# Convolutional attention block, one core: vectors placed by products, two loads moved to SP's queue, and three taps moved behind a Newton step

## The chip, the cores and the metric

The kernel runs on one core of one Trainium2 chip. The time is the device time of the whole program in microseconds (us), as the median of several runs. The engines are TensorE (PE: matrix products; PEld is its weight load), VectorE (DVE), ScalarE (ACT), GpSimd (POOL) and SyncE (SP). DMAs are issued by SP, ACT and POOL.

## What is computed

The reference, cut to the lines that matter (x is 4 x 384 x 48 x 48 in fp32, 8 heads of 48 channels, N = 2304 positions):

```python
local = conv_general_dilated(x, conv_w, ..., feature_group_count=C)   # 7 x 7, depthwise
inv = bn_gamma * rsqrt(bn_var + BN_EPS)
local = local * inv + (bn_beta - bn_mean * inv)
x_norm = layernorm(x_flat, ln_gamma, ln_beta)
q, k, v = split(x_norm @ qkv_w.T + qkv_b)
q = q + layernorm(local_flat, ln_gamma, ln_beta)
attn = softmax(q @ k.T * hd ** -0.5)
out = x_flat + (attn @ v) @ proj_w.T + proj_b
```

## The kernel before

Channels lie on the 128 partitions in three chunks, in a packed order: rows 0 to 47 and 64 to 111 of chunk c hold heads 2c and 2c+1, and rows 48 to 63 and 112 to 127 hold sixteen channels each of the heads 6 and 7. A load into that order takes four DMAs (`load_packed`, L114).

An image has six groups of 384 positions for keys and values (`from_x`), and five groups of 8 or 10 image rows for queries; t counts the query groups over the four images (0 to 19). For each t there are twelve slots s: each scores six blocks of 128 keys (`score`, L1105; each score is three products of high and low parts), exponentiates on ACT (L1113) and sums the values (`weigh`, L1120). The 7 x 7 convolution of group t + 1 runs meanwhile on VectorE, tap by tap (L340), as one long stream; `convolve_first(n)` takes the next n taps of it in the first stage, and `plan` shares out what is left over the slots.

The instructions of TensorE, VectorE, ACT and SP stand in the order in which they are written. GpSimd's order is made by a scheduler after the first loads. A DMA that comes eight after another waits until that one has landed, on the hardware queues (SP and ACT together) and on GpSimd's queue alike.

The first stage (image 0, up to the first score at 163 us) does this:

- SP loads the batch norm vectors (`norms`), the slab (image rows with a border of three) of query group 0 in two parts, between them the weights `staged` of values, keys and queries, and then x of groups 1 to 5 (`load_x`).
- ACT's queue loads the taps (`taps_in`), and with GpSimd's queue the layer norm gain and shift (`of_ln`), piece by piece in packed order (`load_by_pair`, L194 and L196). GpSimd's queue also loads `qk_vec` (bias of queries and keys), `vbp` (bias of values), `pb` (output bias), the slab of group 1 and `w_o`, the output weights. Its scheduler puts one piece of `w_o` and one of the slab among its first instructions.
- `warm` issues 14 products of constants (L1163). Group 0 is then normalised in three blocks: mean (L694), centre on VectorE (L609), squares on ACT (L556), mean of the squares, root on ACT (L617 to L619), a Newton step on VectorE (L631, L632), scale (L689). Between blocks, `pack` (L244) brings taps and shift from natural into packed order by products with 0/1 matrices (`packing`), and ACT copies the result to `vec` (L251).
- `scale_values` and `scale_rows` multiply the weights by the gain (L905, L912, L913). `shift_rows` (L868) makes rows from the layer norm shift and the weights, and `columns` (L894) turns them into columns that are added to the biases (`key_bias`, `query_bias`).
- Groups 1 to 5 follow in a loop; each is normalised one turn ahead. `copies_in` (L361) makes shifted copies of the slab of group 1 with 16 DMAs on SP; `products` (L415, in the turn of group 2) does one chunk of its convolution on TensorE. `stack_head` (L717 to L720, SP) and `stored_head` and its like (L728 to L757, POOL) store the keys. In the last turn (group 5) the norm of the convolved group 0 ends (`local_end`, L942), `query_end` (L954) makes the first queries and `low_queries` (L973) splits them; its DMAs (L978, L980) put the rows where the scores need them.

At t = 0 the queries of t = 1 are made in slot 10: mean of the centred squares on TensorE (L694, after the sums of slot 9), root, Newton step, `local_end`, `query_end`, `low_queries` with six DMAs on SP.

Of the kernel before, what the change touches and what calls it, by code (L numbers as in the profile page):

```python
# [10 lines left out]
F32 = mybir.dt.float32  # L11
# [5 lines left out]
P = 128  # L17
NH = 8
HD = 48
# [29 lines left out]
def unshifted_pass(  # L49
# [16 lines left out]
    nc = tc.nc  # L66
    B, C, N = x.shape
    W = 48
    H = N // W
    CC = C // P  # L70
# [3 lines left out]
    NP = NH // 2  # L74
# [6 lines left out]
    GM = max(ROWS) * W  # L81
# [11 lines left out]
    const = ctx.enter_context(tc.tile_pool(name="const", bufs=1))  # L93
# [12 lines left out]
    def two_banks(name="r"):  # L106
        return ps.tile([P, 2, 512], F32, tag="r", name=name)
# [4 lines left out]
    def load_packed(dst, src, queue=nc.sync):  # L112
        for p0, piece in segments(src):
            queue.dma_start(out=dst[p0 : p0 + piece.shape[0]], in_=piece)  # L114
# [30 lines left out]


    T0 = KS * KS
    natural = work.tile([P, GM], F32, tag="qt", name="natural", bufs=1)[:, 0 : CC * (T0 + 1)]
    natural = natural.rearrange("p (c v) -> p c v", c=CC)
    norms = const.tile([P, 4, CC], F32, tag="norms", name="norms")  # L150
    vec = const.tile([P, CC, T0 + 1], F32, tag="vec", name="vec")
    cw, shift = vec[:, :, 0:T0], vec[:, :, T0]
    of_ln = const.tile([P, 2, CC], F32, tag="of_ln", name="of_ln")
    gain, beta = of_ln[:, 0], of_ln[:, 1]
    inv = const.tile([P, CC], F32, tag="inv", name="inv")
    neg_half = const.tile([P, CC], F32, tag="neg_half", name="neg_half")
    qk_vec = const.tile([P, 2, CC], F32, tag="qk_vec", name="qk_vec")
# [29 lines left out]
    taps_in = piece(CC, T0)  # L187
    nc.scalar.dma_start(out=taps_in, in_=conv_w)

    def load_by_pair(dst, src, queues):  # L190
        with nc.allow_non_contiguous_dma(reason="a few vectors, once"):
            for j, queue in enumerate(queues):
                r = 64 * j
                queue.dma_start(out=dst[r : r + HD], in_=src[j, :, :, 0:CC])  # L194
                for c in range(CC):
                    queue.dma_start(  # L196
                        out=dst[r + HD : r + 64, :, c], in_=src[j, 16 * c : 16 * c + 16, :, CC]
                    )

    load_by_pair(of_ln, ln_pair, (nc.scalar, nc.gpsimd))  # L200
    staged = [
        work.tile([P, CC, GM], F32, tag="qs", name="staged", bufs=5)[:, :, :C] for _ in range(3)
    ]
# [22 lines left out]
    for c, r, cc, r0, n in pieces:  # L226
        nc.vector.tensor_copy(
            packing[:, pairs.index((c, cc)), r : r + n], ident[:, r0 : r0 + n]
        )

    nc.vector.tensor_mul(inv, inv, norms[:, 0])
    nc.vector.tensor_mul(natural[:, :, T0], norms[:, 2], inv)
    nc.vector.tensor_sub(natural[:, :, T0], norms[:, 1], natural[:, :, T0])
# [3 lines left out]
        )  # L237

    def pack():
        m = two_banks()[:, 0, 0 : CC * (T0 + 1)].rearrange("p (c v) -> p c v", c=CC)  # L240
        for c in range(CC):
            mine = [pair for pair in pairs if pair[0] == c]
            for pair in mine:
                nc.tensor.matmul(  # L244
                    m[:, c, :],
                    lhsT=packing[:, pairs.index(pair), :],
                    rhs=natural[:, pair[1], :],
                    start=pair == mine[0],
                    stop=pair == mine[-1],
                )  # L250
        nc.scalar.copy(vec, m)  # L251
# [13 lines left out]
    ]  # L265
    for g in range(1, NG):
        load_x(0, g, nc.sync)
    load_by_pair(qk_vec, qk_b, (nc.gpsimd, nc.gpsimd))
    with nc.allow_non_contiguous_dma(reason="a few vectors, once"):
        load_packed(vbp, v_b.rearrange("o c -> c o"), nc.gpsimd)  # L270
    nc.gpsimd.dma_start(out=pb, in_=proj_b)
    loads.close()

# [583 lines left out]
    rows = {}  # L859

    def of_row(i):
        return slice(32 * i, 32 * i + 1)

    def shift_rows():
        r = two_banks()
        for c in range(CC):
            for i in range(3):
                nc.tensor.matmul(  # L868
                    r[of_row(i), 0, :C],
                    lhsT=beta[:, c : c + 1],  # L870
                    rhs=staged[i][:, c, :],
                    start=c == 0,
                    stop=c == CC - 1,
                )
        rows.update((i, r[of_row(i), 0, :C]) for i in range(3))

    def rows_out():
# [36 lines left out]

    def key_bias(m):
        nc.vector.tensor_add(qkb[:, 1, :], qk_vec[:, 1, :], m[1])
        nc.vector.tensor_add(vbp[:, :, 0], vbp[:, :, 0], m[2])

    def query_bias(m):

# [232 lines left out]
    def convolve_first(n):  # L1153
        nonlocal n_first
        n_first += n
        for _ in range(n):
            next(stream)


    def warm(n):  # L1160
        m = two_banks()[:, 0, 0:P]
        for _ in range(n):
            nc.tensor.matmul(m, lhsT=mean_w, rhs=ident, start=True, stop=True)  # L1163

    warm(WARM)

    blocks = [slice(i * P, (i + 1) * P) for i in range(NB)]
    raw = slabs[0, 0][0]
# [5 lines left out]
    for i, at in enumerate(blocks):  # L1174
        norm.mean_of(norm.buf, at)
        norm.root(at)
        norm.scale(norm.newton(at), at)
        scale_values(*((0,), (1, 2), ())[i])
        if i == 1:
            pack()  # L1180
            convolve_first(2)
    for c in range(CC):
        scale_rows(1, c)
# [21 lines left out]
    convolve_first(5)  # L1205
    norm.mean_by_chunk(norm.buf)
    norm.root()
    load_slab(0, 1)
    load_packed(w_o, proj_wT, nc.gpsimd)
    both(making)  # L1210
    convolve_first(4)
    lows_out(1)
# [7 lines left out]
    for g in range(1, NG):  # L1220

        last = g == NG - 1
        making = from_x(0, g)
        both(making)
        if last:
            added = output_bias()
        else:
            norm.mean_in_place()
            convolve_first(6)
        if g in (3, 5):  # L1230
            keep_stack(0, g // 2 - 1)
        norm.centre()
        norm.squares()
        if last:
            convolve_first(3)
            norm.sum_squares()
            convolve_first(3)
        both(making)
        if last:
            norm.mean_in_place()  # L1240
        else:
            if g == 1:
                taps_out()
            if g == 2:
                products()
                convolve_first(24)
            convolve_first(5)
            norm.sum_squares()
            both(making)
            norm.mean_in_place()  # L1250
        norm.root()
        if last:
            convolve_first(9)
            local_end(0, norm.newton())
            query_end(0, True)
            both(making)
            low_queries(0, 0, nc.scalar)
            convolve_first(2)
            lows_out(1)
            both(making)  # L1260
            convolve_first(4)
            both(making)
            continue
        lows_out(1)
        both(making)
        convolve_first(6)
        lows_out(2)
        norm.scale(norm.newton())
        if g == 1:
            taps_spread()  # L1270
        both(making)
        if g == NG - 2:
            assert n_first >= each
            norm = Norm(accs[0])
            norm.mean_by_chunk(norm.src)
        if g < NG - 2:
            norm = Norm(xn[0, g + 2])
            norm.sum()
        convolve_first(5)
# [6 lines left out]
    for t in range(NT):  # L1286
# [74 lines left out]
        for s in range(NSLOT):  # L1361
# [64 lines left out]
                between.extend(norm.root_jobs())  # L1426
                between.popleft()()
            if early and s == first + (2 if t == 0 else 3):
                low_queries(t + 1, 0)
            convolve("slot", t, s, 1)  # L1430
            if t and early and s == first + 2:
                local_end(t + 1, norm.newton())
# [588 lines left out]
```

## Time and profile before

| | before |
|---|---|
| median of 3 runs | 2739.66 us (2739.60 to 2740.39) |
| profiled execution | 2739.04 us |
| its span | 2737.2 us |
| TensorE / VectorE / ACT / GpSimd busy | 2714.7 / 2314.8 / 1671.1 / 603.9 us |
| matmuls | 16438 records |
| HBM read / written | 258.14 / 64.14 MB |

The profile is of one execution. Busy time counts the instructions of an engine; a matmul of fp32 data makes two records. Timelines give start and length in us, the engine, the line of the kernel, the operation, out<-in with partitions and elements, and in brackets the idle time before it and what ended it. A line can be that of a helper (L694 is `project`, L114 `load_packed`), so the names tell the instructions apart.

### The profile page before, as it was taken

The page shows a single profiled execution, that of the slowest core. Times are in us where ns is not written, and L with a number is a line of the kernel's source. Part 1 is how long each engine was busy: PE and PEld are TensorE (multiplying, and loading weights), DVE is VectorE, ACT ScalarE, POOL GpSimd, SP SyncE. Part 2 cuts the span into 40 slices and gives each one's busy share as a digit, 9 for nine tenths or more (in the row PEclk, how much of TensorE's full clock was granted, in tenths as well). Part 3 has the DMA queues.
Part 4 walks back from the last instruction along what each step waited for, and adds up shares of the span by engine and source line. Part 5 has one row for each costly group of instructions (what it writes and reads, how often), then busy time and mean ns, then how long its engine had stood idle before and what let it go on. Part 6 is the DMA issues. An engine that isn't in the chain of part 4 may idle for free.

```text
span 2737.2 us, 46047 instructions
## 1 busy us (share of the span) xinstructions
PE 2714.7 (99%) x16438; PEld 1536.6 (56%) x16438; DVE 2314.8 (85%) x4038; ACT 1671.1 (61%) x2317; POOL 603.9 (22%) x1077
## 2 busy tenths in 40 slices
PE   8999999999999999999999999999999999999999
PEld 5565555555556555555555655555555565555555
DVE  7999999989999999989889999889888998986212
ACT  4356777777325777777622677777752377776762
POOL 5541101102453111011155211111225511110110
PEclk9999999999999999999999999999999999999999
DMA  8354544446465545354555553545635544444442
GB/s 164 85 143 136 142 115 129 124 136 182 101 160 154 139 120 146 115 152 124 143 140 138 166 147 110 142 126 141 152 105 158 147 140 133 139 132 132 139 150 68
DMA packets 160223, 370.46 MB, mean 135 GB/s; under 512 B 58672, under 2 KB 107472, under 8 KB 159984
## 3 DMA queue, kind: packets, MB, share of 16 engines
q0 software_dynamic: 71424, 279.04, 35.6%
q1 hardware_dynamic: 83248, 78.33, 12.6%
q10 hardware_dynamic: 5312, 10.06, 1.1%
q8 instruction: 132, 2.16, 0.3%
q14 instruction: 107, 0.88, 0.1%
HBM read 258.14 MB, written 64.14 MB: 118 GB/s over the span
## 4 chain that ended last, share of the span: by engine, by line
PE 90%; DVE 5%; DMA 4%; ACT 0%; issue 0%; SPq 0%; POOL 0%; DVEq 0%; POOLq 0%; ACTq 0%
PE o L1120 42%; PE r L1105 34%; PE r L694 13%; DVE acc L340 2%; DMA parts<-part 1%; DMA staged<-in_qkv_wT_dram 1%; DVE k L804 0%; DMA slab<-in_x_dram 0%; PE r L415 0%; DMA four<-parts 0%; DVE xn L689 0%; DMA wide<-k 0%; DMA xn<-in_x_dram 0%; DMA out_dram<-xr 0%; DVE xr L1086 0%
## 5 line engine op out<-in xcount | busy, mean ns | idle before, releaser
L340 DVE SCALAR_TENSOR_TENSOR acc<-slab,vec,acc 128x470 f32<-128x470 f32 (+10 forms) x2832 | 1658.1, 658 | 2.0 <-ACT acc L303 2.0
L1113 ACT ACTIVATE pt<-r 128x960 f32<-128x960 f32 (+1 forms) x1440 | 1248.6, 943 | 246.4 <-PE o L1120 151.8
L1120 PE MATMUL o<-pt,v 128*64 128x480 f32 (+1 forms) x5760 | 1166.2, 554 | 0.4 <-ACT pt L1113 0.4
L1105 PE MATMUL r<-qs,ks 64*128 64x480 f32 (+1 forms) x8640 | 967.0, 373 | 4.8 <-ACT xn L818 3.0
L1105 PEld LDWEIGHTS r<-qs,ks 64*128 64x128 f32 x8640 | 785.2, 184 | 268.2 <-issue 171.6
L1120 PEld LDWEIGHTS o<-pt,v 128*64 128x64 f32 x5760 | 392.5, 137 | 659.9 <-issue 566.5
L766 POOL DMA_DIRECT2D ks<-wide x220 | 160.0, 727 | 1369.7 <-PE r L1105 1310.0
L694 PE MATMUL r<-xn,w_qk 128*128 128x384 f32 x864 | 284.7, 487 | 0.0
L997 ACT COPY o<-o 113x480 f32<-113x480 f32 (+1 forms) x160 | 87.1, 544 | 277.3 <-PE o L1120 276.7
L694 PEld LDWEIGHTS r<-xn,w_qk 128*128 128x128 f32 x864 | 164.4, 191 | 115.3 <-issue 1.8
L694 PE MATMUL r<-w_v,xn 128*128 128x384 f32 x432 | 145.3, 489 | 2.8 <-DVE xn L689 1.4
L788 ACT COPY v<-r 128x384 f32<-128x384 f32 x72 | 32.0, 479 | 183.3 <-PE r L694 183.3
L1016 DVE TENSOR_TENSOR ao<-ao,o 113x480 f32<-113x480 f32 (+1 forms) x120 | 75.9, 633 | 73.9 <-ACT o L997 73.9
L694 PEld LDWEIGHTS r<-w_v,xn 128*128 128x128 f32 x432 | 81.1, 190 | 62.6 <-DVE xn L689 3.8
L973 DVE TENSOR_TENSOR qs<-xn,qs 128x480 fp32r<-128x480 f32 (+1 forms) x60 | 38.1, 635 | 63.8 <-ACT qs L968 63.8
L751 POOL DMA_DIRECT2D wide<-k x144 | 72.4, 505 | 78.3 <-ACT k L801 64.2
L694 PE MATMUL r<-af,w_o 128*128 128x384 f32 (+1 forms) x270 | 85.2, 470 | 0.0
L1007 ACT COPY ao<-o 113x480 f32<-113x480 f32 (+1 forms) x60 | 32.6, 544 | 72.1 <-PE o L1120 72.1
L1016 DVE TENSOR_TENSOR aot<-aot,o 113x480 f32<-113x480 f32 (+1 forms) x40 | 25.4, 634 | 56.9 <-ACT o L997 56.9
L818 ACT ACTIVATE xn<-r,qkb 128x384 f32<-128x384 f32 x72 | 39.6, 576 | 50.8 <-PE r L694 47.6
L1086 DVE SCALAR_TENSOR_TENSOR xr<-r,pb,xr 128x384 f32<-128x384 f32 (+2 forms) x72 | 42.0, 611 | 33.2 <-PE r L694 26.0
L694 PEld LDWEIGHTS r<-af,w_o 128*128 128x128 f32 x270 | 51.3, 190 | 31.9
(148 smaller groups left out, 1354.9 us busy)
## 6 DMA issues: line engine op xcount, KB each, us to landing
ks<-wide POOLq DMA_DIRECT2D x220, 768.0 KB, 4.9
qs<-qs SPq DMA_DIRECT2D x352, 60.0 KB
slab<-in_x_dram POOLq DMA_DIRECT2D x24, 432.0 KB, 7.2
wide<-k POOLq DMA_DIRECT2D x96, 96.0 KB, 2.2
wide<-ks POOLq DMA_DIRECT2D x12, 768.0 KB, 5.3
xr<-in_x_dram POOLq DMA_DIRECT2D x16, 576.0 KB, 5.6
rb<-rden SPq DMA_DIRECT2D x32, 270.0 KB
held<-ao POOLq DMA_DIRECT2D x12, 720.0 KB, 3.9
```

What stands on the lines that cost most here:

```text
L340: nc.vector.scalar_tensor_tensor(dst, src, weight, dst, ALU.mult, ALU.add)
L694: nc.tensor.matmul(dst, lhsT=weights(c), rhs=src(c), start=c == 0, stop=c == CC - 1)
L751: nc.gpsimd.dma_start(out=last[16 * u : 16 * u + 16, 0], in_=k[r : r + 16, 0])
L766: queue.dma_start(out=place_keys(b, p, i), in_=wide[b, p][:, :, at])
L818: nc.scalar.activation(src[:, i, :], q[:, :G], AF.Identity, bias=qkb[:, 0, i : i + 1])
L973: nc.vector.tensor_sub(qs[:, 1, :], query_of(t, p), qs[:, 0, :])
L997: nc.scalar.copy(part[0 : 64 + HA], sums[0 : 64 + HA, 0, :n])
L1016: nc.vector.tensor_add(dst, dst, part[0 : 64 + HA])
L1086: nc.vector.scalar_tensor_tensor(xr[:, co, :], m, pb[:, co : co + 1], xr[:, co, :], ALU.add, ALU.add)
L1105: nc.tensor.matmul(r[:, j, :n], lhsT=ks[rows, w, at], rhs=qs[rows, m, :], start=i == 0, stop=i == 2,)
L1113: nc.scalar.activation(pt, r[:, :, :n], AF.Exp, scale=SCALE)
L1120: nc.tensor.matmul(sums[halves[j], 0, : columns_of(t)], lhsT=values[t // NA, kb // NB][:, first : first + 64], rhs=pt[:, j, :], start=i == ...
```

## The change

It does six things. The layer norm vectors, the query and key biases and the value bias are loaded by contiguous rows on ACT's queue into a corner of the start-up buffer, and `proj_b` moves to ACT's queue as well. Gain and shift become two more columns of `natural`, which `pack` places with the taps (52 columns instead of 50 a chunk); `pack` moves ahead of the first norm, right behind `warm`. `bias_rows` (VectorE) builds 0/1 rows and `bias_out` (four products and a copy on ACT) places the query and key biases. The value bias is added as one more product at the end of `shift_rows`. The slab of group 1 moves from GpSimd's queue to SP's, behind x of group 2, and `w_o` to SP's behind x of group 5. In the last turn of the first stage the taps ahead of the Newton step go from 9 to 6, those behind it from 2 + 4 to 3 + 6; and at t = 0 half of the DMAs of `low_queries` for t = 1 go to GpSimd's queue instead of SP's.

```diff
--- before.py
+++ after.py
@@ -145,13 +145,12 @@
 
 
     T0 = KS * KS
-    natural = work.tile([P, GM], F32, tag="qt", name="natural", bufs=1)[:, 0 : CC * (T0 + 1)]
+    natural = work.tile([P, GM], F32, tag="qt", name="natural", bufs=1)[:, 0 : CC * (T0 + 3)]
     natural = natural.rearrange("p (c v) -> p c v", c=CC)
     norms = const.tile([P, 4, CC], F32, tag="norms", name="norms")
-    vec = const.tile([P, CC, T0 + 1], F32, tag="vec", name="vec")
+    vec = const.tile([P, CC, T0 + 3], F32, tag="vec", name="vec")
     cw, shift = vec[:, :, 0:T0], vec[:, :, T0]
-    of_ln = const.tile([P, 2, CC], F32, tag="of_ln", name="of_ln")
-    gain, beta = of_ln[:, 0], of_ln[:, 1]
+    gain, beta = vec[:, :, T0 + 1], vec[:, :, T0 + 2]
     inv = const.tile([P, CC], F32, tag="inv", name="inv")
     neg_half = const.tile([P, CC], F32, tag="neg_half", name="neg_half")
     qk_vec = const.tile([P, 2, CC], F32, tag="qk_vec", name="qk_vec")
@@ -187,17 +186,13 @@
     taps_in = piece(CC, T0)
     nc.scalar.dma_start(out=taps_in, in_=conv_w)
 
-    def load_by_pair(dst, src, queues):
-        with nc.allow_non_contiguous_dma(reason="a few vectors, once"):
-            for j, queue in enumerate(queues):
-                r = 64 * j
-                queue.dma_start(out=dst[r : r + HD], in_=src[j, :, :, 0:CC])
-                for c in range(CC):
-                    queue.dma_start(
-                        out=dst[r + HD : r + 64, :, c], in_=src[j, 16 * c : 16 * c + 16, :, CC]
-                    )
-
-    load_by_pair(of_ln, ln_pair, (nc.scalar, nc.gpsimd))
+    of_ln = piece(2, CC)
+    nc.scalar.dma_start(out=of_ln, in_=ln)
+    biases = piece(2, NP)
+    nc.scalar.dma_start(out=biases[0 : 2 * HD], in_=qk_b.rearrange("j d v p -> (j d) v p"))
+    of_values = piece(C)[64:65]
+    nc.scalar.dma_start(out=of_values, in_=v_b)
+    nc.scalar.dma_start(out=pb, in_=proj_b)
     staged = [
         work.tile([P, CC, GM], F32, tag="qs", name="staged", bufs=5)[:, :, :C] for _ in range(3)
     ]
@@ -228,6 +223,7 @@
             packing[:, pairs.index((c, cc)), r : r + n], ident[:, r0 : r0 + n]
         )
 
+    nc.vector.tensor_copy(natural[:, :, T0 + 1 : T0 + 3], of_ln.rearrange("p v c -> p c v"))
     nc.vector.tensor_mul(inv, inv, norms[:, 0])
     nc.vector.tensor_mul(natural[:, :, T0], norms[:, 2], inv)
     nc.vector.tensor_sub(natural[:, :, T0], norms[:, 1], natural[:, :, T0])
@@ -237,7 +233,7 @@
         )
 
     def pack():
-        m = two_banks()[:, 0, 0 : CC * (T0 + 1)].rearrange("p (c v) -> p c v", c=CC)
+        m = two_banks()[:, 0, 0 : CC * (T0 + 3)].rearrange("p (c v) -> p c v", c=CC)
         for c in range(CC):
             mine = [pair for pair in pairs if pair[0] == c]
             for pair in mine:
@@ -265,11 +261,40 @@
     ]
     for g in range(1, NG):
         load_x(0, g, nc.sync)
-    load_by_pair(qk_vec, qk_b, (nc.gpsimd, nc.gpsimd))
-    with nc.allow_non_contiguous_dma(reason="a few vectors, once"):
-        load_packed(vbp, v_b.rearrange("o c -> c o"), nc.gpsimd)
-    nc.gpsimd.dma_start(out=pb, in_=proj_b)
+        if g == 2:
+            load_slab(0, 1, queue=nc.sync)
+    load_packed(w_o, proj_wT)
     loads.close()
+
+    chosen_rows = spread_taps[1][:, 2 * 448 : 2 * 448 + 4 * P].rearrange("p (a m) -> p a m", m=P)
+
+    def bias_rows():
+
+        rows = chosen_rows.rearrange("p a (j x) -> p a j x", j=2)
+        nc.vector.memset(chosen_rows, 0.0)
+        nc.vector.tensor_copy(
+            rows[:, 0, :, 0:HD], ident[:, 0 : 2 * HD].rearrange("p (j d) -> p j d", j=2)
+        )
+        nc.vector.tensor_copy(
+            rows[:, 1:4, :, HD:64],
+            ident[:, 0 : 2 * HD].rearrange("p (j c r) -> p c j r", j=2, c=CC),
+        )
+
+    def bias_out():
+        m = two_banks()[:, 0, 0 : 2 * CC].rearrange("p (v c) -> p v c", v=2)
+        rows = slice(0, 2 * HD)
+        nc.tensor.matmul(
+            m, lhsT=chosen_rows[rows, 0, :], rhs=biases[rows, :, 0:CC], start=True, stop=False
+        )
+        for c in range(CC):
+            nc.tensor.matmul(
+                m[:, :, c],
+                lhsT=chosen_rows[rows, 1 + c, :],
+                rhs=biases[rows, :, CC],
+                start=False,
+                stop=c == CC - 1,
+            )
+        nc.scalar.copy(qk_vec, m)
 
 
 
@@ -870,8 +895,11 @@
                     lhsT=beta[:, c : c + 1],
                     rhs=staged[i][:, c, :],
                     start=c == 0,
-                    stop=c == CC - 1,
+                    stop=c == CC - 1 and i != 2,
                 )
+        nc.tensor.matmul(
+            r[of_row(2), 0, :C], lhsT=one[of_row(2)], rhs=of_values, start=False, stop=True
+        )
         rows.update((i, r[of_row(i), 0, :C]) for i in range(3))
 
     def rows_out():
@@ -914,7 +942,7 @@
 
     def key_bias(m):
         nc.vector.tensor_add(qkb[:, 1, :], qk_vec[:, 1, :], m[1])
-        nc.vector.tensor_add(vbp[:, :, 0], vbp[:, :, 0], m[2])
+        nc.vector.tensor_copy(vbp[:, :, 0], m[2])
 
     def query_bias(m):
 
@@ -1163,6 +1191,8 @@
             nc.tensor.matmul(m, lhsT=mean_w, rhs=ident, start=True, stop=True)
 
     warm(WARM)
+    pack()
+    bias_rows()
 
     blocks = [slice(i * P, (i + 1) * P) for i in range(NB)]
     raw = slabs[0, 0][0]
@@ -1177,7 +1207,7 @@
         norm.scale(norm.newton(at), at)
         scale_values(*((0,), (1, 2), ())[i])
         if i == 1:
-            pack()
+            bias_out()
             convolve_first(2)
     for c in range(CC):
         scale_rows(1, c)
@@ -1205,8 +1235,6 @@
     convolve_first(5)
     norm.mean_by_chunk(norm.buf)
     norm.root()
-    load_slab(0, 1)
-    load_packed(w_o, proj_wT, nc.gpsimd)
     both(making)
     convolve_first(4)
     lows_out(1)
@@ -1250,15 +1278,15 @@
             norm.mean_in_place()
         norm.root()
         if last:
-            convolve_first(9)
+            convolve_first(6)
             local_end(0, norm.newton())
             query_end(0, True)
             both(making)
             low_queries(0, 0, nc.scalar)
-            convolve_first(2)
+            convolve_first(3)
             lows_out(1)
             both(making)
-            convolve_first(4)
+            convolve_first(6)
             both(making)
             continue
         lows_out(1)
@@ -1426,7 +1454,7 @@
                 between.extend(norm.root_jobs())
                 between.popleft()()
             if early and s == first + (2 if t == 0 else 3):
-                low_queries(t + 1, 0)
+                low_queries(t + 1, 0, nc.gpsimd if t == 0 else nc.sync)
             convolve("slot", t, s, 1)
             if t and early and s == first + 2:
                 local_end(t + 1, norm.newton())
```

## Prediction

> **What bounds the kernel now.** The page first: TensorE is busy nearly all the time, so a change pays only where TensorE is idle, runs at a reduced clock, or has work taken away.
>
> ```profile
> span 2737.2 us, 46047 instructions
> PE 2714.7 (99%) x16438; PEld 1536.6 (56%) x16438; DVE 2314.8 (85%) x4038; ACT 1671.1 (61%) x2317; POOL 603.9 (22%) x1077
> ```
>
> 2737.2 - 2714.7 = 22.5 us of idle time. The waits of TensorE (total, times, longest) say that over half of it lies before 165 us:
>
> ```profile
> PE r L1105 <- ACT xn L818: 3.0, 1, 3.0
> PE r L1163 <- POOL mean_w L165: 2.8, 1, 2.8
> PE r L694 <- DMA xn<-in_x_dram: 2.8, 1, 2.8
> PE r L694 <- issue: 2.5, 1, 2.5
> ```
>
> The timeline of TensorE places them (start, length; in brackets the idle time before and its releaser):
>
> ```profile
> 10.60 3.70 PE L694 MATMUL r<-slab,mean_w 128*128 128x128 f32 x18 [2.50 <-issue]
> 14.14 1.50 PE L694 MATMUL r<-sq,mean_w 128*128 128x128 f32 x12
> 15.48 1.66 PE L244 MATMUL r<-natural,start_up 128*128 128x50 f32 x14
> 26.41 2.10 PE L694 MATMUL r<-xn,w_qk 128*128 128x384 f32 x6
> 32.53 4.18 PE L694 MATMUL r<-xn,mean_w 128*128 128x384 f32 x6 [2.76 <-DMA xn<-in_x_dram]
> 36.50 4.56 PE L694 MATMUL r<-xn,w_qk 128*128 128x384 f32 x12
> ```
>
> Six records of 128x384 take 2.10 us at 26.41 and 4.18 at 32.53: after each idle stretch the clock is halved. The table by stretch of time has it (third column from the end is the clock):
>
> ```profile
> 10.00:12.00 2.00, 1.40 (x6) 1.43 (x7) 0.00 (x0) 0.00 (x0) 1.01 (x2) 0.56 1.11 156
> 32.00:34.00 2.00, 1.47 (x3) 0.90 (x4) 0.77 (x2) 0.00 (x0) 1.02 (x2) 0.50 1.03 189
> ```
>
> The last two columns are DMA, saturated at 156 to 189 GB/s: two loads hold TensorE up, the fourth piece of the first slab (0,0) and group 1 of x. VectorE waits with it (3.97 us, then 1.36 us):
>
> ```profile
> 36.74 0.16 DVE L921 TENSOR_TENSOR qkb<-qk_vec,r 128x3 f32<-128x3 f32 x1 [3.97 <-PE r L694]
> 44.82 0.62 DVE L631 SCALAR_TENSOR_TENSOR sq<-r,eps,sq 128x384 f32<-128x384 f32 x1 [1.36 <-ACT sq L619]
> ```
>
> GpSimd's timeline shows who shares the DMA engines: loads that nobody needs before 47.9 us (the slab of group 1) and 143 us (w_o):
>
> ```profile
> 1.44 0.74 POOL L114 DMA_DIRECT2D w_o<-in_proj_wT_dram  x1 [0.38 <-issue]
> 5.06 0.65 POOL L114 DMA_DIRECT2D slab<-in_x_dram  x1
> ```
>
> [...] in the first 12 us GpSimd's queue takes 36.9% of the engines and SP's 47.4%. [...] 674 of the 1552 packets of those 12 us are under 512 B. [...] here 2.50 and 2.76 us were enough and 0.93 us (at 259.4) was not, so I use the trace.
>
> **The change, part by part.**
>
> Fewer DMAs ahead (POOL). GpSimd loses 25 issues; ACT keeps five, all contiguous rows now. Bytes ahead of x group 1 on SP: slab 576 KB, weights 1728, slab's rest 216, x 576: 3.17 MB. GpSimd adds 1152 + 576 KB = 1.77 MB. At 165 GB/s (table, 12 to 24 us) from 2.0 us: 21.2 us alone, 31.9 with GpSimd's; it landed at 32.4. So group 1 should land near 22 to 23 us. The slab: its fourth piece is issued at 5.08, when the first has landed, and lands at 10.5; 648 KB of w_o and slab lie between, up to 4 us, so it should land at 6.5 to 8.
>
> Start of TensorE. The mean weights come after one DMA issue less (0.74) and five memsets more (0.37): 0.4 earlier. The warm-up (5.31) ends at 7.7. pack() now comes here, 1.66 us, to 9.35. It needs `natural`, ready at 7.74 before; its chain was behind 2.1 us of GpSimd issues, now gone, and two vectors on ACT's queue. bias_rows (memset by the 896-column one's 0.81 us: 0.46; two copies, up to 0.4) fits VectorE's 4.53 us of waiting. So the means start at 9.35 instead of 10.60 (-1.25) with no idle gap: 18 warm records take 2.25 (by 12 in 1.50) instead of 3.70 (-1.45, of which I take 1.25, since VectorE and ACT follow in steps). At ACT's first root: **-2.5**.
>
> To the columns (end 29.76). ACT is full there; it loses the 0.26 us vec copy and gains a smaller one. TensorE: pack's 1.66 gone; bias_out 4 x 0.24 (pack's mean) and the v row 2.33/9 = 0.26 added, 1.2: no loss. The four vbp DMAs and the addition vanish. Columns end at 27.3 to 27.5.
>
> Group 1. x is there, so its mean starts at 27.5, not 32.53: -5.0. No gap, so warm: 2.10 for 4.18, 4.1 for 4.56: another -2.5. The mean of the squares then starts at 33.7 instead of 40.90. VectorE's 22 taps end at 32.77 - 2.5 = 30.3, centre by 32.0, ACT's squares end at 33.2: in time. **-7.2**, for VectorE too (newton 44.82 to about 37.5). Bounds: 4 (one of the gaps or cold stretches stays) to 9.
>
> 46 to 147 us. TensorE has no gap over 0.42 us, VectorE hardly any; both are shifted alike. Later uses: group 2 at 48.4 - 7.2 = 41 (lands by 27), the copies of slab 1 by products() at 77.84 - 7.2 = 70.6 (below), w_o at 136. SP's 8 further loads cover bytes that landed by 42 us anyway. Nothing is added.
>
> 9 taps to 6. Total taps ahead of the loop stay at 21, and VectorE is without a gap from 147.0 to 243.5. The first queries leave 3 x 0.62 = 1.86 us earlier and the 3.44 us of idle before the first scores (162.95, 163.98) shrink to 1.6, perhaps with the cold stretch behind it (clock 0.50 at 165 to 167). But the same taps follow, and the next meeting point is tight:
>
> ```profile
> 239.93 2.68 PE L694 MATMUL r<-sq,mean_w 128*128 128x480 f32 x6
> 237.59 1.65 DVE L609 TENSOR_TENSOR acc<-acc,sq 128x1440 f32<-128x1440 f32 x1
> ```
>
> ACT's first square is done at 239.8, TensorE takes it at 239.93. Coming 2 us early it waits 2 us. I take **-0.1**; bounds 0 and -2.7.
>
> Queries of t = 1 on two queues. SP's last three DMAs leave from 253.93 and meet the key load of 254.83:
>
> ```profile
> 254.57 1.22 SPq L980 DMA_DIRECT2D qs<-qs  x2
> 260.32 3.70 PE L1105 MATMUL r<-qs,ks 64*128 64x480 f32 x31 [0.93 <-DMA qs<-qs]
> ```
>
> In the order of instructions GpSimd's three stand behind the key load of 246.98, ahead of that of 254.83; they wait for VectorE's low part (252.05), take 0.5 us each, and land 2.0 to 2.3 us later (its `wide` writes of like size): 256, before 258.47. **-0.93**. Behind them only that key load could slip, by nothing. Bounds: 0 and -1.0.
>
> Sum: -7.2 - 0.1 - 0.93 = -8.2. The profiled execution took 2739.04 (1.84 around its span), 0.62 under the median: 2730.8 for it, **2731.4** as a median.
>
> **Rivals.** (a) The early gain is partly handed back: a gap remains at the first mean because a vector lands late on ACT's queue, or a cold stretch survives. For it: TensorE and VectorE alternate as bound from 46 us on. Against: the DMA arithmetic that reproduces 32.4. Gain 3 to 5.4: 2735.5. (b) The 2 us of the earlier queries survive because ACT's squares or VectorE come earlier too; against it VectorE has no wait there: 2729. (c) **Slower: SP's queue becomes the bound.** SP now issues 28 loads, 8 key moves (5 us) and 16 copies (10.6 us) in a row before products(). Before, 20 loads took 20.3 us from 20.1. At 1.0 us each the copies land at 66, at 1.2 us they are just late (70.6). At 1.8 us each: 20.1 + 50.4 + 15.6 + 2 = 88.1, 10.3 us behind 77.84, less 0.93: 2749. It decides from 1.66 us per load on, where 5.5 us are lost; the engines' rate of 165 GB/s or more speaks against it. (d) The change does nothing measurable: x and slab come late for SP's own sake (eight of its DMAs in flight). Then only the 0.93 and 1 to 2 us of pack remain: 2737.5.
>
> **The numbers.** 0.2%, 5.5 us, is about what a measurement can tell from no change. Main case 0.64 (gain 6 to 10), b 0.13, a 0.13, d 0.05, c 0.05. Faster 0.77, same 0.18 (a, d), slower 0.05. The range leaves out c, d and the tail of b: 2727.0 to 2736.5.
>
> **What would show it.** Right: pack before the slab's mean; no gap over 1 us and clock 1.0 from 2.4 to 46 us; xn,mean_w near 27.5 in 2.1 us; values of group 1 at 41.4 instead of 48.64; the gap before t = 1's scores gone; a new gap of up to 2 us before the mean at 240 - 7. Wrong: a DMA named as releaser of group 1's mean, or of products(), or values of group 1 later than 44.

## The result and the profile after

| | before | after |
|---|---|---|
| median (6 runs each, same chip) | 2740.47 us (2739.60 to 2741.27) | 2729.14 us (2728.42 to 2732.13) |
| ratio, 95% interval | | 0.9960 (0.9948 to 0.9973) |
| profiled execution, span | 2739.04, 2737.2 us | 2728.42, 2726.5 us |

The change saves 11.3 us by the medians and 10.7 us by the spans of the two traces; 8.2 were predicted. It is a gain of 0.4%, small, but the interval of the ratio lies clear of 1. The page after begins so (busy time, share of the span, instructions):

```profile
span 2726.5 us, 46025 instructions
PE 2712.0 (99%) x16448; PEld 1533.7 (56%) x16448; DVE 2315.1 (85%) x4042; ACT 1671.5 (61%) x2318; POOL 590.3 (22%) x1055
```

TensorE's idle time went from 22.5 to 2726.5 - 2712.0 = 14.5 us, 8.0 less; its busy time fell by 2.7 us although it has ten records more: some work that had run at half the clock no longer does. The waits of TensorE (total, times, longest) show what is left:

```profile
PE r L1133 <- DMA qs<-qs: 2.0, 2, 1.9
PE r L1191 <- POOL one L167: 1.8, 1, 1.8
PE r L1133 <- DVE k L829: 1.5, 2, 0.9
```

Neither x nor the slab is among them. New at the top is a wait for queries. TensorE's timeline for the start (start, length, records, idle time before):

```profile
1.81 5.64 PE L1191 MATMUL r<-ident,mean_w 128*128 128x128 f32 x28 [1.81 <-POOL one L167]
7.29 1.66 PE L240 MATMUL r<-natural,start_up 128*128 128x52 f32 x14
8.79 2.24 PE L719 MATMUL r<-slab,mean_w 128*128 128x128 f32 x18
...
26.69 2.20 PE L719 MATMUL r<-xn,mean_w 128*128 128x384 f32 x6
28.73 4.03 PE L719 MATMUL r<-xn,w_qk 128*128 128x384 f32 x12
32.60 2.10 PE L719 MATMUL r<-sq,mean_w 128*128 128x384 f32 x6
...
40.34 4.03 PE L719 MATMUL r<-w_v,xn 128*128 128x384 f32 x12
```

The slab's mean follows on `pack` with no bracket (no idle time), and group 1's mean on the columns with none: it stands at 26.69 instead of 32.53, and its six records take 2.20 us instead of 4.18. The table by stretch of time (third column from the end: granted clock; then the DMA share and GB/s) has the clock at 1.00 where it was 0.56 and 0.50:

```profile
10.00:12.00 2.00, 2.00 (x20) 1.95 (x19) 1.38 (x3) 1.40 (x3) 0.00 (x0) 1.00 1.10 187
32.00:34.00 2.00, 2.00 (x8) 1.21 (x7) 2.00 (x6) 1.22 (x3) 0.33 (x1) 1.00 1.11 193
```

The DMA engines are as full as before (a share of 1.10 and 1.11 in these two stretches, 1.11 and 1.03 in the kernel before); what comes first over them is different. SP's queue has it (the loads of x are now ahead of the slab of group 1, and w_o is last):

```profile
14.91 5.50 SPq L114 DMA_DIRECT2D xn<-in_x_dram  x8
20.45 1.97 SPq L114 DMA_DIRECT2D slab<-in_x_dram  x4
23.14 13.22 SPq L114 DMA_DIRECT2D xn<-in_x_dram  x12
37.03 2.29 SPq L114 DMA_DIRECT2D w_o<-in_proj_wT_dram  x4
```

The fourth of those slab loads is the eighth DMA behind the fourth piece of x of group 1, and it waits for that piece's semaphore. The semaphore was complete at 22.01 and the load left at 22.02, so x was there over 4 us before TensorE wanted it. In the kernel before, x of group 1 landed at 32.39. VectorE gets to group 1's Newton step at 36.52 instead of 44.82:

```profile
36.52 0.62 DVE L656 SCALAR_TENSOR_TENSOR sq<-r,eps,sq 128x384 f32<-128x384 f32 x1 [0.61 <-ACT sq L644]
```

**How the gain travels.** The trace can be read as a ledger: take one instruction at several places and see how much earlier it starts than in the kernel before.

| place | before | after | earlier |
|---|---|---|---|
| ACT's first root | 15.36 | 12.08 | 3.28 |
| mean of group 1 (xn,mean_w) | 32.53 | 26.69 | 5.84 |
| Newton step of group 1 | 44.82 | 36.52 | 8.30 |
| first scores | 162.95 | 152.52 | 10.43 |
| means in slot 9 | 239.93 | 231.60 | 8.33 |
| first scores of t = 1 | 258.47 | 250.14 | 8.33 |
| weighing behind them | 263.95 | 254.24 | 9.71 |
| span | 2737.2 | 2726.5 | 10.7 |

8.30 is won by 44 us; 2.1 more by the first scores, which is taken back by slot 9; and 1.4 stays with the queries of t = 1. In the kernel before, the first scores and VectorE's low part of the third pair of heads stood so:

```profile
162.95 0.62 PE L1105 MATMUL r<-qs,ks 64*128 64x384 f32 x4 [3.03 <-ACT xn L818]
163.98 4.59 PE L1105 MATMUL r<-qs,ks 64*128 64x384 f32 x32 [0.41 <-DMA qs<-qs]
...
198.65 0.55 DVE L973 TENSOR_TENSOR qs<-xn,qs 128x384 fp32r<-128x384 f32 x1
```

TensorE's timeline after, around the first score and the third pair of heads shows where the 2.1 went:

```profile
152.52 0.82 PE L1133 MATMUL r<-qs,ks 64*128 64x384 f32 x4 [0.91 <-DVE k L829]
...
201.46 3.04 PE L1133 MATMUL r<-qs,ks 64*128 64x384 f32 x31 [1.85 <-DMA qs<-qs]
...
231.60 2.68 PE L719 MATMUL r<-sq,mean_w 128*128 128x480 f32 x6
```

The wait before the first scores fell from 3.03 to 0.91 us. In its place TensorE stands 1.85 us ahead of 201.46. The third pair's queries come late, because VectorE reaches their low part only behind the taps, and still at the same distance from the Newton step (153.8 us in both kernels):

```profile
190.33 0.55 DVE L1001 TENSOR_TENSOR qs<-xn,qs 128x384 fp32r<-128x384 f32 x1
```

Their six DMAs leave one behind the other on SP's queue; the last left at 194.18 and landed at 201.32.

From group 1's Newton step to slot 9's means the old kernel takes 239.93 - 44.82 = 195.11 us, the new one 231.60 - 36.52 = 195.08. That distance is the marker for the experiments: a shift of the first stage leaves it alone, and moving taps has to alter it in order to be worth anything.

### The profile page after: what moved, and what is told of

It reads as the page before. It is cut to its first block, busy times and chain, and to the rows that moved or that the text cites. A ratio compares the mean times of both kernels' runs of the same rounds, so it can differ in the third digit from the quotient of the medians.

```text
span 2726.5 us, 46025 instructions
## 1 busy us (share of the span) xinstructions
PE 2712.0 (99%) x16448; PEld 1533.7 (56%) x16448; DVE 2315.1 (85%) x4042; ACT 1671.5 (61%) x2318; POOL 590.3 (22%) x1055
## 4 chain that ended last, share of the span: by engine, by line
PE 87%; DVE 7%; DMA 4%; issue 0%; ACT 0%; SPq 0%; POOL 0%; DVEq 0%; POOLq 0%
PE o L1148 41%; PE r L1133 34%; PE r L719 11%; DVE acc L365 4%; DMA four<-parts 1%; DMA xn<-in_x_dram 1%; DMA parts<-part 1%; DVE k L829 1%; DMA staged<-in_qkv_wT_dram 0%; DMA wide<-k 0%; DVE xn L714 0%; DMA slab<-in_x_dram 0%; DVE xr L1114 0%; DMA qs<-qs 0%; PE r L618 0%
## 5 line engine op out<-in xcount | busy, mean ns | idle before, releaser
L843 ACT ACTIVATE xn<-r,qkb 128x384 f32<-128x384 f32 x72 | 39.7, 578 | 50.9 <-PE r L719 47.4
```

What stands on the lines that cost most here:

```text
L843: nc.scalar.activation(src[:, i, :], q[:, :G], AF.Identity, bias=qkb[:, 0, i : i + 1])
```

## The experiments

**Theory.** The first 8.3 us come from the order of the loads alone (slab of group 1 and w_o behind x on SP's queue). The taps are worth nothing where they were put, because VectorE has no gap from 138.6 us until the means of slot 9. The second queue for t = 1 is worth 0.9 to 1.4 us. **Rivals.** The vectors by rows, or `pack` ahead of the mean, carry part of the first stage; the clock, not the wait, carries it; the taps themselves bring the later microseconds.

In the table, "Newton" is group 1's step, "means" those of slot 9, all in us. The ratio is to the kernel before on the same chip. Single executions of the kernel before lay between 2732 and 2742 us, so the traces' markers separate smaller effects than the medians do.

| kernel | Newton | first scores | means | means - Newton | span | median (runs) | ratio, 95% |
|---|---|---|---|---|---|---|---|
| before | 44.82 | 162.95 | 239.93 | 195.11 | 2737.2 | see above | |
| after | 36.52 | 152.52 | 231.60 | 195.08 | 2726.5 | 2729.14 (6) | 0.9960 (0.9948 to 0.9973) |
| e1_queue_only | 36.00 | 154.15 | 231.26 | 195.26 | 2727.9 | 2729.77 (6) | 0.9971 (0.9959 to 0.9983) |
| e2_loads_back | 46.03 | 162.05 | 241.14 | 195.11 | 2734.3 | 2738.48 (12) | 1.0001 (0.9993 to 1.0010) |
| e3_pack_back | 36.53 | 152.55 | 231.63 | 195.10 | 2726.2 | 2728.26 (5) | 0.9966 (0.9953 to 0.9979) |
| e4_taps_back | 35.79 | 153.61 | 230.90 | 195.11 | 2726.6 | 2728.50 (5) | 0.9962 (0.9949 to 0.9976) |
| e5_sp_queries | 36.36 | 152.37 | 232.06 | 195.70 | 2730.1 | 2730.54 (22) | 0.9980 (0.9973 to 0.9986) |
| e6_taps_gap | 36.51 | 151.53 | 228.38 | 191.87 | 2721.4 | 2724.06 (5) | 0.9958 (0.9945 to 0.9971) |
| e7_warm_gap | 41.69 | 159.86 | 237.59 | 195.90 | 2733.1 | 2735.45 (12) | 0.9997 (0.9989 to 1.0006) |
| e8_slab_first | 44.03 | 160.40 | 239.47 | 195.44 | 2733.9 | 2734.81 (12) | 0.9990 (0.9982 to 0.9998) |
| e9_no_vectors | 35.78 | 150.80 | 227.65 | 191.87 | 2723.9 | 2723.17 (5) | 0.9951 (0.9937 to 0.9965) |

### The queue alone, and all but the queue

e1_queue_only is the kernel before with the two loads moved, and nothing else of the change:

```diff
     for g in range(1, NG):
         load_x(0, g, nc.sync)
+        if g == 2:
+            load_slab(0, 1, queue=nc.sync)
+    load_packed(w_o, proj_wT)
...
     norm.root()
-    load_slab(0, 1)
-    load_packed(w_o, proj_wT, nc.gpsimd)
```

> The kernel before with one part of the change: slab of group 1 and w_o on SP's queue behind x. Theory A (the 1.77 MB that GpSimd's queue sent beside x and the first slab made both gaps): most of the first stage's 8.3 us comes back; Newton step of group 1 at 38 to 39.5 us (before 44.8, after 36.5), no DMA named ahead of group 1's mean, time 2733 to 2735. Rival B (the vectors' element-sized pieces filled the DMA engines and the queues): Newton at 43 or later, time 2739 or more.

TensorE's timeline of e1:

```profile
8.25 2.25 PE L697 MATMUL r<-slab,mean_w 128*128 128x128 f32 x18 [1.00 <-issue]
...
26.16 2.20 PE L697 MATMUL r<-xn,mean_w 128*128 128x384 f32 x6
...
154.15 0.62 PE L1108 MATMUL r<-qs,ks 64*128 64x384 f32 x4 [3.05 <-DMA qs<-qs]
155.19 4.71 PE L1108 MATMUL r<-qs,ks 64*128 64x384 f32 x32 [0.42 <-DMA qs<-qs]
```

Group 1's mean comes at 26.16, warm (2.20 us, as at the full clock), without a wait; the Newton step at 36.00 is even 0.5 us ahead of the full change, and 2 us earlier than the 38 to 39.5 that had been expected, because the earlier start came back with it as well. The slab's mean has 1.00 us of waiting left, behind which its 18 records run warm (2.25 us). The wait before the first scores is the old one, 3.05 us with the cold stretch behind it (32 records in 4.71 us), and yet slot 9 comes at 231.26: what was lost at 154 was no loss by 231.

e2_loads_back is the reverse: the whole change, with these two loads back on GpSimd's queue where they stood.

> The kernel after with the slab of group 1 and w_o back on GpSimd's queue, all else kept. Nothing stands ahead of them there now, so all eight DMAs leave in the first 8 us. Theory A: group 1 of x lands at about 32 us again (same bytes ahead of it), the first slab lands later than in either kernel (11 to 14 us), Newton step of group 1 at 44 to 47 us; time 2737 to 2741. Rival B: Newton at 40 or earlier, time 2733 or less.

TensorE's timeline of e2:

```profile
12.55 4.18 PE L716 MATMUL r<-slab,mean_w 128*128 128x128 f32 x18 [2.33 <-issue]
...
36.20 2.20 PE L716 MATMUL r<-xn,mean_w 128*128 128x384 f32 x6
```

The slab is late again (2.33 us, then 18 records in 4.18 us, as at the halved clock, where e1 took 2.25), Newton stands at 46.03, and the median is that of the kernel before. The first-stage gain is in where these two loads stand in the queues, and all of it. But e2 isn't the kernel before in detail: all eight pieces left GpSimd between 1.4 and 7.8 us, the first slab landed at 12.46 (10.51 in the kernel before), and group 0 came so late that the mean of group 1, at 36.20, had no wait for x. So e2 shows the cost to the first slab; the cost to x is shown by e8, below.

### pack back behind the means

```diff
     warm(WARM)
-    pack()
     bias_rows()
...
         norm.squares(at)
+    pack()
     for i, at in enumerate(blocks):
```

> The kernel after with pack() behind the three means of group 0 instead of ahead of them. Theory A: pack's 1.66 us only fills the wait for the slab; behind the means it stands ahead of the means of the squares, which VectorE and ACT pace with a step of 1.5 us, so it costs 0 to 1 us; Newton of group 1 at 36.5 to 37.5, time 2729 to 2730. Rival: the early place is worth the whole 1.7 us or more (a gap at 7.5 us brings the halved clock back): Newton at 38.2 or later, 2731 or more.

TensorE's timeline of e3:

```profile
7.55 2.17 PE L719 MATMUL r<-slab,mean_w 128*128 128x128 f32 x18
9.56 1.66 PE L240 MATMUL r<-natural,start_up 128*128 128x52 f32 x14
...
200.65 3.04 PE L1133 MATMUL r<-qs,ks 64*128 64x384 f32 x31 [1.01 <-DMA qs<-qs]
...
231.63 2.68 PE L719 MATMUL r<-sq,mean_w 128*128 128x480 f32 x6 [0.80 <-ACT sq L586]
```

The slab's last piece was there by 7.55, so in this execution there was no gap for `pack` to fill; its place is worth 0.0 (Newton 36.53 to 36.52). The last two lines show most of the 2.1 us handed back in two portions here, 1.01 us at the third pair and 0.80 us at the means.

### The taps

e4_taps_back keeps the old 9, 2 and 4 taps:

```diff
-            convolve_first(6)
+            convolve_first(9)
...
-            convolve_first(3)
+            convolve_first(2)
...
-            convolve_first(6)
+            convolve_first(4)
```

> The kernel after with 9 taps ahead of the last Newton step of the first stage and 2 and 4 behind, as before. Theory A (VectorE without a gap from 139 to 235 us sets the pace there, so TensorE's earlier start is handed back): first scores at 154.4 instead of 152.5, but the wait of 1.85 us for the third pair's queries at 199.6 shrinks to nothing, and the sums of slot 9 end at the same 231.6; time 2729.1, within 0.7. Rival: the earlier start is kept: 2731 or more.

TensorE's timeline of e4:

```profile
153.61 0.87 PE L1133 MATMUL r<-qs,ks 64*128 64x384 f32 x4 [2.72 <-DVE acc L365]
154.66 4.81 PE L1133 MATMUL r<-qs,ks 64*128 64x384 f32 x32 [0.18 <-DMA qs<-qs]
```

The first scores wait 2.72 us for VectorE's `acc` and then run cold (32 records in 4.81 us; the granted clock was 0.50 from 156 to 158 us), which is what the change had taken away. Slot 9 still comes 195.11 us behind Newton, against 195.08 with the taps moved: the step is worth nothing. It moves the wait. None of the five traces with the old taps (the kernel before twice, e1, e4, e7) has a wait at the third pair; all six with the change's taps have one, of 0.99 to 2.48 us. Either place can cost: e7, with the old taps, came to 195.90 by a cold stretch at its first scores (36 records in 6.37 us, the granted clock 0.50 from 160 to 164 us), and e5 and e11, with the new, to 195.70 and 196.54 by the third pair.

VectorE does have a wait in which taps would cost nothing, earlier in the same turn. In the timeline of VectorE after:

```profile
138.60 0.56 DVE L591 TENSOR_TENSOR sq<-sq 128x384 f32<-128x384 f32 x1 [3.88 <-ACT sq L581]
```

e6_taps_gap puts six more taps there and leaves three each at three of the four places behind it (the fourth, just behind the sum of squares, has three already); the sum over the places named is 18 as before:

```diff
-            convolve_first(3)
+            convolve_first(9)
             norm.sum_squares()
...
-            convolve_first(6)
+            convolve_first(3)
             local_end(0, norm.newton())
...
-            convolve_first(6)
+            convolve_first(3)
```

> The kernel after with the same 21 taps, six of them moved into VectorE's wait of 3.88 us at 134.7 us: 9 ahead of the sum of squares instead of 3, then 3, 3, 3 and 3. Theory A (VectorE's order of work decides when TensorE may use its early start): VectorE is 3.0 to 3.3 us earlier from 157 us on, the waits before and after the first scores (0.91, 0.63 us) and the one for the third pair's queries (1.85 us) go, the means of slot 9 come at 228.3 instead of 231.6; time 2725.5 to 2726.5. Rival (the DMA engines' load, not VectorE, makes the queries late): the wait at 199.6 stays and the gain is under 1 us.

VectorE's timeline of e6:

```profile
132.84 5.61 DVE L365 SCALAR_TENSOR_TENSOR acc<-slab,vec,acc 128x450 f32<-128x450 f32 x9
138.59 0.56 DVE L591 TENSOR_TENSOR sq<-sq 128x384 f32<-128x384 f32 x1
```

The same instruction stands at 138.59 instead of 138.60, with six more taps done and no bracket. Slot 9 comes 3.2 us earlier (191.87 behind Newton), the waits at the first scores and at the third pair are gone, and the span of this execution is 5.1 us shorter. VectorE is without a gap only from 138.6 us on: taps moved into the gap ahead of it are worth something, while taps moved behind it are not. It also answers the rival that the DMA engines' load makes the third pair late: with VectorE 3.2 us earlier, the wait is gone.

### The queries of t = 1 on one queue

e5_sp_queries leaves all six DMAs on SP:

```diff
-                low_queries(t + 1, 0, nc.gpsimd if t == 0 else nc.sync)
+                low_queries(t + 1, 0)
```

> The kernel after with all six DMAs of the queries of t = 1 on SP's queue, as before. Theory A: the wait of 0.9 us ahead of the first scores of t = 1 is back (at about 251 us) and nothing else changes: time 0.9 to 1.4 us above the kernel after, 2730.0 to 2730.5. Rival: the last DMA lands in time anyway, since everything is shifted: 2729.1.

TensorE's timeline of e5:

```profile
253.78 3.71 PE L1133 MATMUL r<-qs,ks 64*128 64x480 f32 x31 [2.27 <-DMA qs<-qs]
```

The wait that the change removed is back, and larger. In the five traces with one queue it was 0.93 (before), 1.20 (the kernel before once more, below), 0.95 (e1), 2.25 (e7) and 2.27 us (e5). The traces with two queues have none there. The product behind it (the weighing) starts at 257.41, 3.2 us later than after the change; 0.5 of that was there at slot 9 already, from a wait of 2.48 us at the third pair. The median, 2730.54, lies at the upper end of what was expected.

### The wait or the clock

e7_warm_gap is the kernel before with seven products of constants in the gap ahead of group 1's mean, so that x is as late as before and TensorE isn't idle for long:

```diff
+    warm(7)
     norm.mean_by_chunk(norm.src, bank)
```

> The kernel before with seven products of constants (2.66 us) in TensorE's wait for group 1 of x. Theory A: x still lands at 32.4, but the mean (4.18 us) runs at the full clock, 2.1 us, and the twelve records behind it in 4.1 for 4.56: Newton of group 1 at 42.3 to 42.6 instead of 44.8, time 2737.5 to 2738.5. Rival (only the wait costs; the halved clock is hidden behind VectorE and ACT): 2740.

TensorE's timeline of e7:

```profile
31.89 2.17 PE L694 MATMUL r<-xn,mean_w 128*128 128x384 f32 x6 [0.30 <-DMA xn<-in_x_dram]
```

Six records take 2.17 us instead of 4.18, and the twelve behind them 4.03 instead of 4.56: about 2.5 us of the gain at this place is the clock, as in the change itself (8.30 - 5.84 = 2.46). Newton came 3.1 us earlier, more than expected, because x landed 0.6 us earlier in this execution (31.75 for 32.39). The slab's mean also ran warm (18 records in 2.25 us), but had no part in it: the columns ended at 29.83, in the kernel before at 29.76. The ratio cannot tell the kernel from the one before.

### The slab ahead of x

e8_slab_first leaves both loads on SP but puts the slab of group 1 ahead of x of group 1:

```diff
     for g in range(1, NG):
+        if g == 1:
+            load_slab(0, 1, queue=nc.sync)
         load_x(0, g, nc.sync)
-        if g == 2:
-            load_slab(0, 1, queue=nc.sync)
```

> The kernel after with the slab of group 1 ahead of x of group 1 on SP's queue instead of behind group 2. Theory A: x of group 1 landed by 22.1 us (SP's fourth slab load could leave then) and was needed at 26.7, so it had 4.6 us to spare; 1.18 MB ahead of it at 195 GB/s are 6.05 us, so its mean starts at about 28.1, 1.4 us late: Newton at 37.5 to 38.2, time 2730 to 2731. Rival (the order on the queue counts in full): 6 us, 2735. Rival (no effect): 2729.

TensorE's timeline of e8:

```profile
32.44 3.97 PE L719 MATMUL r<-xn,mean_w 128*128 128x384 f32 x6 [5.42 <-DMA xn<-in_x_dram]
```

The order on the queue decides, not the queue's name: the start is as early as after the change, and yet the wait for x is back at 5.42 us, with the cold stretch (the granted clock was 0.50 from 30 to 34 us). It is longer than expected, because the slab's 1.18 MB held x up for about 10 us (it landed at 32.34 instead of 22.01), which makes 114 GB/s by estimate, not the 195 that the expectation had worked with. Newton stands at 44.03, 7.5 us later than after the change: x alone can cost nearly the whole of the first stage's gain.

### Without the vectors

e9_no_vectors is the kernel before with the queue (the diff of e1), the taps of e6 and the second queue for t = 1. The vectors are loaded and `pack` stands as in the kernel before.

> The kernel before with the two loads on SP's queue, half of the queries' DMAs of t = 1 on GpSimd's, and the taps in VectorE's wait (9, 3, 3, 3, 3); the vectors, pack and the biases are left as before. Theory A (the queue move is the whole of the first stage; the vectors by rows and the early pack are worth nothing): Newton of group 1 at 36.0 to 36.6, the means of slot 9 195.1 - 3.2 = 191.9 us behind it, no wait ahead of t = 1; time 2724.1 within 0.8, like the same taps with the vectors by rows. Rival (the vectors by rows keep the queues free later on, or the early pack counts): 1.5 us or more above that.

VectorE's and TensorE's timelines of e9:

```profile
35.78 0.62 DVE L634 SCALAR_TENSOR_TENSOR sq<-r,eps,sq 128x384 f32<-128x384 f32 x1 [0.65 <-ACT sq L622]
...
227.65 2.68 PE L697 MATMUL r<-sq,mean_w 128*128 128x480 f32 x6 [0.90 <-ACT sq L564]
```

Newton 35.78, means 227.65, 191.87 apart; the median is 2723.17. All that e6 has is there without the vectors by rows, `bias_rows`, `bias_out` and the early `pack`: that part of the change, most of its lines, brings nothing that these runs show.

### The same kernels once more

The kernel before on another chip; then the kernel after and e6's version side by side on a third:

> The kernel before once more, for a second trace of its first stage. Theory A: group 1 of x lands late again (31 to 33 us), the means run at the halved clock behind the gap, Newton of group 1 at 43 to 45 us, slot 9's means 195.1 us behind it; what moves from execution to execution is the landing of x and the wait ahead of t = 1 (0.9 to 2.3 us). Rival (the first trace was an outlier): Newton under 41 us.

> The kernel after once more, beside the next one on the same chip. Theory A: Newton of group 1 at 35.8 to 36.6, slot 9's means 195.1 us behind it, ratio to before 0.996; the wait for the third pair's queries is 1 to 2 us or, where it is shorter, the rest of it stands ahead of slot 9's means. Rival (the 10.7 us between the first two traces were partly chance): ratio 0.998.

> The kernel after with the six taps in VectorE's wait once more, beside the kernel after on the same chip. Theory A: 3.2 us of the first 230 us are kept to the end, so its median is 2.5 to 4.5 us under that of the kernel after. Rival (later meeting points take it back): under 1 us.

The kernel before took 2740.7 us (one run, span 2738.9, Newton 45.27, 195.13 to slot 9), as in its first trace; x landed at 33.64. After: 2727.59 us (6 runs, 0.9967, 0.9955 to 0.9979); e6's version: 2725.72 us (5 runs, 0.9957, 0.9944 to 0.9970). Newton stood at 36.95 and 37.01, slot 9 at 233.49 and 228.88, the spans were 2727.5 and 2723.6. The distance after was 196.54, outside of what was expected, for a reason that its timeline shows:

```profile
201.82 4.59 PE L1133 MATMUL r<-qs,ks 64*128 64x384 f32 x31 [1.77 <-DMA qs<-qs]
```

The wait at the third pair is as long as in the first trace (1.77 and 1.85 us), but this time the granted clock dropped behind it (0.51 and 0.50 from 202 to 204 us, 1.00 in the first trace), and the 31 records took 4.59 instead of 3.04 us: 1.55 us, about the 1.46 by which 196.54 exceeds 195.08. By the traces e6's version is 3.9 us ahead of the change; by the medians on this chip it is 1.9 us ahead, with intervals that overlap, less than the 2.5 to 4.5 that were expected and more than its rival's 1. The change itself is 10.6 us ahead of the kernel before on this chip. So e6's version and e9, which has its taps, are the fastest that were run, but how far they are ahead of the change end to end is not settled.

## Why the prediction was right, and where its terms were off

- **Fewer DMAs ahead, x at 22 to 23.** Right. x had landed by 22.0. With the two loads back on GpSimd's queue (e2) the gain is gone, there by way of the first slab; with the slab ahead of x (e8) the wait for x is back.
- **Start of TensorE, -2.5.** It was 3.28 at ACT's first root. The products of constants began 0.99 us earlier, where 0.4 was put (1.81 for 2.80), but took 5.64 us instead of 5.31; they ended at 7.45, not 7.7, `pack` began 0.16 before that, and so the mean began at 8.79, not 9.35: 1.81 instead of 1.25. ACT then took over the other 1.47 us of the warm products whole, where 1.25 was allowed. The reason given to `pack` was wrong: it was not needed as a filler, since the slab was there at 7.55 (e3).
- **Group 1's mean at 27.5, warm.** 26.69, in 2.20 us. The columns ended 0.5 to 0.7 us earlier than put (26.76), an outcome of the earlier start. The values of group 1 came at 40.34, not 41.4. In sum the first stage gave **8.3 instead of 7.2**: the warm records brought the 2.5 that was put (8.30 - 5.84 = 2.46), and the mean started 5.84 earlier instead of 5.0. The prediction's own two terms make 7.5, not 7.2: it set the two stretches of records end to end, 2.10 and 4.1, where they overlap in the trace (2.20 and 4.03 us of records lie between 26.69 and 32.60, which is 5.91).
- **46 to 147 us, nothing.** Right: 8.30 at 44.82, and 8.31 at 146.91 (VectorE's L566, now L591 at 138.60).
- **9 taps to 6, -0.1, handed back.** Right in size (0.0 by e4), and right that the first scores gain about 2 us and lose them at a tight meeting point (a place where TensorE needs what VectorE has just made). It named only the means of slot 9. The first meeting point is the third pair's queries, 30 us sooner; e3 and e6 show the named one as well (0.80 and 1.08 us of waiting for ACT's squares).
- **Queries of t = 1, -0.93.** It was 1.38 between the two traces: the old kernel's batch took 263.95 - 258.47 = 5.48 us with its wait, the new one 4.10. The step took the wait of one execution for a constant; it varies from 0.93 to 2.27.
- **Sum.** 8.3 + 0.0 + 1.4 = 9.7, where 8.2 was put. The span gained another 1.0 us in the later turns, where two waits of the kernel before (1.04 us at 817.66, 1.32 at 2146.93) have no counterpart in the trace after. e3 and e9 have such waits again (1.04 us at 809.19; 1.05 at 804.66), so they come and go between executions; no run was made for them, and this 1.0 stays open. The measured gain, 10.7 to 11.3 us, lies above the 6 to 10 of the main case. The time still fell into the stated range, because the range reached down to 2727.0 for rival (b), which did not happen: the mechanism of the first stage was right, the nearness of the time to rival (b)'s is luck.
- **Rivals.** (a), a gap or a cold stretch that remains, did not come about. (b), the queries' 2 us survive, fits the time (2729) but not the trace: they were handed back, and the extra is in the terms above. (c), SP's queue as the bound, was clear of deciding: its loads were issued by 39.3 us, and `products` came 8.31 us earlier (69.53 for 77.84), as did all around it. (d) would have had x late on SP's queue as well, and it was not.

## What to carry to other kernels

Where the DMA engines are full, ask for each load by when it is needed, and put those with time to spare behind the urgent ones on the same queue: on another queue they share the engines however late their work is (in the first 12 us of the kernel before, GpSimd's queue took 36.9% of the engines beside SP's 47.4%). Where an engine has no gap up to the next meeting point, moving its work back within that stretch buys a start that is given back there; look for the engine's own waits and move the work into them. A wait of 2 us may cost nearly as much again in clock behind it (1.77 and 1.55 us in e11), so count the records after it, too.

## What the runs showed of the hardware

The length of a gap alone didn't decide whether TensorE's clock halved around it. The records behind the gap ran at the halved clock at 1.04 us (e2, at 21.52: 12 records in 6.03 us, 4.11 in e1), 1.77 (e11, below), 2.23 (e10: 18 records in 3.87 us, 2.25 in e1) and 2.33 (e2: the same 18 in 4.18). The granted clock stayed at 1.00 at 1.85 (after), 2.25 (e7), 2.27 and 2.48 us (e5). At each gap of 2.50 us and more in the start and at the first scores, behind the first products, it halved, by the granted clock or by the time that the records took: 2.50, 2.76 and 3.03 us in the kernel before, 2.72 in e4, 3.05 in e1, 3.08 in e7, 3.05 and 3.18 in e10, 5.42 in e8. The table by stretch of time has the 1.77 us case of e11:

```profile
201.00:202.00 1.00, 0.18 (x2) 0.21 (x4) 1.00 (x3) 0.00 (x0) 1.00 (x3) 1.00 0.25 37
202.00:203.00 1.00, 1.00 (x8) 1.00 (x9) 1.00 (x3) 0.60 (x1) 1.00 (x3) 0.51 0.80 160
```

and that of e5, after 2.48 us:

```profile
202.00:204.00 2.00, 2.00 (x24) 2.00 (x25) 2.00 (x5) 1.55 (x3) 1.00 (x2) 1.00 1.00 187
```

In the trace of the kernel before, the clock was halved from 10.24 to 13.65 us, from 30.72 to 37.55 and from 163.84 to 167.25, at the gaps of 2.50, 2.76 and 3.03 us, and at no other time between 0 and 2730 us. What decides at a gap of 1 to 2.5 us was not shown.
